# A grouped convolution with quantised weights: another order of loads, statistics and step sizes at the beginning

## The chip, the cores and the metric

The kernel runs on one core of a Trainium2 chip. The metric is the device time of one execution in microseconds (us); for each kernel several executions are timed and their median is compared. One execution is also recorded by the hardware profiler, and all lines of a profile come from that one.

## What is computed

The input `x` is 160 images of 128 channels by 32 x 32. Each image is normalised over groups of four channels, then convolved (3 x 3, padding 1, 128 channels to 128), and the result is added to the image itself. There are five weight sets; in the reference image m uses set m mod 5, and the kernel sorts the images so that it has 32 per set. The weights are quantised in two steps whose sizes come from the range of all five sets together:

```python
beta, alpha = jnp.max(U), jnp.min(U)
s1 = (beta - alpha) / 3.0
v1 = s1 * floor(U / s1)
s2 = s1 / 5.0
v2 = s2 * floor((U - v1) / s2)
w = (v1 + v2).reshape(128 * 5, 128, 3, 3)
act = conv_general_dilated(gn(x).reshape(32, 5 * 128, 32, 32), w, padding 1, feature_group_count=5)
out = x + act.reshape(160, 128, 32, 32)
```

So no weight can be quantised before all five sets have been read, and no convolution can start before the first weights are quantised.

## The kernel before

All channels lie on the 128 partitions. An image is split into a high and a low fp16 part (`high_part` L521, `low_part` L579), and TensorE multiplies both with the weights. The weights of a set are made in three columns (`make_column` L446), one for each horizontal tap, in the order 1, 0, 2 (`COLS`, L344); below they are the first, second and third column. The program is written out by hand: each engine runs its own instructions strictly in the order in which the Python code emits them, and waits at an instruction until what it reads is there.

The order of the beginning, in `run` (L774):

- **Loads** (L779 to L790), all issued by SyncE on one queue. Set 0 goes to `u0` in two halves of 288 KB, sets 1 to 4 go whole (576 KB) to `range1` to `range4`, image buffers that are given back after the range is known. Then follow images 0 to 3, one by one (512 KB, L414), and pairs of images (1024 KB, L411). The compiled program has eight landing counters for this queue and takes them in turn: its ninth transfer is issued once the first has landed, its eleventh once the third has, and so on.
- **Range** (`weight_range`, L420). VectorE takes the maximum (L426) and the minimum (L427) of each piece as it arrives, six pieces of 1, 1, 2, 2, 2 and 2 halves, then joins them (`ext1`, L431). `over_partitions` (L434) finds the extremes over the partitions: two transposes on TensorE (L439), a maximum on VectorE (`top`, L441) and a product with ones (`spread`, L443).
- **Step sizes** (`from_range`, L50): VectorE operations on 128 x 1 values. `span` (L74); `s1` by four operations (L58 to L61); four numbers from s1, called its parts (L66 to L71: minus s1, its reciprocal, and the two pieces of minus s1); `s2` by four operations from s1 (L58 to L61 again); `lift` (L78); the parts of s2. The loop at L832 puts them in turn with the operations of the first column: eight of these small ones come before the column's first operation, `nn` (L99), which needs the reciprocal of s1.
- **Columns**: thirteen operations on 128 x 384 values from `nn` to the second integer part (L112), then six products on TensorE that turn the column round (`pt`, L467), then ScalarE writes the weights (`wt`, L480). The second and the third column have their first operation on ScalarE (`ns`, L99).
- **Statistics** of images 0 and 1, and of 2 and 3, group by group. ScalarE sums an image (L192) and its squares (L199) into `mv`; TensorE averages over the channel group (`means`, L208); ScalarE copies (`ngm`, L217); four GpSimd operations make `dv` (L219 to L222); TensorE averages again (`variances`, L225); ScalarE (`ve`, L231) and GpSimd (L235 to L244) make `rstd` and `shift`, for which `lift` is needed (L239). Then ScalarE writes `z` (L515) and the high part `hi` (L523), and VectorE the low part `lo` (L581).
- **Dummy products** (`warm_up`, L636): products of zeros on TensorE, 14 between the means and the variances of images 2 and 3, and 7 after the first column's `pt`.
- **First three images**: TensorE takes the high parts of images 0, 1, 2 and then their low parts with the first column (L866 to L869: 36 products, L621). The second column's `pt` stands behind these 36 in TensorE's order. The 36 products with the second column follow, with the third column's `pt` among them, and then the third column.

The lines that set the order around the change:

```python
spread = self.over_partitions(self.weight_range(list(self.us.values())), ident)
...
for ahead in (8, 1, 1, 1, 1, 1, 3, 1, 1, 1):
    take(chain, ahead)
    take(first, 1)
run(chain)
measure(0, 0, 1)
measure(1, 0, 1)
self.stats[0].means()
```

Of the kernel before, what the change touches and what calls it, by code (L numbers as in the profile page):

```python
# [33 lines left out]
class Steps:  # L34
# [12 lines left out]
    def col(self, tag, dt=F32):  # L47
        return self.pool.tile([self.nc.NUM_PARTITIONS, 1], dt, tag=tag, name=tag)

    def from_range(self, extg):  # L50


        nc, col = self.nc, self.col

        def divide_exact(tag, q1, a, m):

            q0, rem = col(tag + "q0"), col(tag + "rem")
            yield nc.vector.tensor_scalar_mul(q0, a, 1.0 / m)  # L58
            yield nc.vector.scalar_tensor_tensor(rem, q0, -(m - 1.0), a, ALU.mult, ALU.add)
            yield nc.vector.tensor_sub(rem, rem, q0)  # L60
            yield nc.vector.scalar_tensor_tensor(q1, rem, 1.0 / m, q0, ALU.mult, ALU.add)  # L61

        def parts(out, s):

            r, neg, hi, lo = out
            yield nc.vector.tensor_scalar_mul(neg, s, -1.0)  # L66
            yield nc.vector.reciprocal(r, s)
            yield nc.vector.tensor_single_scalar(
                hi.bitcast(I32), neg.bitcast(I32), -4096, op=ALU.bitwise_and
            )  # L70
            yield nc.vector.tensor_sub(lo, neg, hi)  # L71

        span = col("span")
        yield nc.vector.tensor_reduce(span, extg, AX.X, ALU.add)  # L74
        yield from divide_exact("s1", self.s1, span, 3.0)
        yield from parts(self.parts1, self.s1)
        yield from divide_exact("s2", self.s2, self.s1, 5.0)
        yield nc.vector.tensor_scalar_mul(self.lift, self.s2, LIFT)  # L78
        yield from parts(self.parts2, self.s2)
        self.span, self.big = span, col("big")  # L80
        yield nc.vector.tensor_reduce(self.big, extg, AX.X, ALU.max)
# [51 lines left out]
def run(steps):  # L133

    while True:
        try:
            next(steps)
        except StopIteration as end:
            return end.value
# [107 lines left out]
def general_path(tc, keep, steps, x, u, out):  # L247
# [8 lines left out]
    with tc.If(far > 0), ExitStack() as ctx:  # L256
# [9 lines left out]
        for n in range(N_SETS):  # L266
            un = one.tile([P, C, TAPS], F32, tag="u", name=f"g_u{n}")
            nc.sync.dma_start(un, uv[n])
            wn = one.tile([P, C, TAPS], F32, tag="w", name=f"g_w{n}")
            k1, k2 = run(steps.quantise(one, un, f"g{n}", F32))  # L270
            nc.vector.tensor_scalar_mul(wn, k1, steps.s1)
            nc.vector.scalar_tensor_tensor(wn, k2, steps.s2, wn, ALU.mult, ALU.add)
# [37 lines left out]
class Main:  # L310
# [109 lines left out]
    def weight_range(self, us):  # L420

        nc, P = self.nc, self.P
        pieces = [us[0][:, : P // 2], us[0][:, P // 2 :], *us[1:]]
        ext = self.const.tile([P, 2, len(pieces)], F32, tag="ext", name="ext")
        for k, piece in enumerate(pieces):
            nc.vector.tensor_reduce(ext[:, 0, k : k + 1], piece, AX.XY, ALU.max)  # L426
            nc.vector.tensor_reduce(  # L427
                ext[:, 1, k : k + 1], piece, AX.XY, ALU.min, negate=True
            )
        ext1 = self.const.tile([P, 2], F32, tag="ext1", name="ext1")  # L430
        nc.vector.tensor_reduce(ext1, ext, AX.X, ALU.max)  # L431
        return ext1

    def over_partitions(self, ext1, ident):  # L434

        nc, P = self.nc, self.P
        rows = self.ps_tr.tile([1, 2, P], F32, tag="pt", name="rows")
        for k in range(2):
            nc.tensor.transpose(rows[:, k, :], ext1[:, k : k + 1], ident)  # L439
        top = self.const.tile([1, 2], F32, tag="top", name="top")  # L440
        nc.vector.tensor_reduce(top, rows, AX.X, ALU.max)  # L441
        spread = self.ps_tr.tile([P, 2], F32, tag="pt", name="spread")
        nc.tensor.matmul(spread, self.ones, top, start=True, stop=True)  # L443
        return spread
# [44 lines left out]
    def by_vector(self, i):  # L489
        return i in self.BY_VECTOR  # L490

    def measure(self, i, stages=(0, 1)):


        k = self.group_of[i]
        g = self.groups[k]
        if k not in self.stats:
            self.stats[k] = Statistics(
                self.nc, self.small, self.ps_stat, self.gavg, self.mhalf, len(g),
                self.steps.lift, k,  # L500
            )
        st, j, image = self.stats[k], i - g.start, self.image(i)
        if self.by_vector(i):
            st.image(j, image)
            return
        for s in stages:
            junk = self.unread.tile([self.P, 1024], MM, tag="junk", name=f"junk{i}_{s}")
            (st.image_sum, st.image_square)[s](j, image, junk)
# [265 lines left out]
    def run(self):  # L774
        nc, P = self.nc, self.P
# [3 lines left out]
        for n in range(N_SETS):  # L779
            if n == 0:  # L780
                un = self.upool.tile([P, P, TAPS], F32, tag="u", name="u0")
            else:
                un = self.space(f"range{n}").rearrange("p j e -> p (j e)")[:, : P * TAPS]
                un = un.rearrange("p (i k) -> p i k", k=TAPS)
            half = P // 2 if n == 0 else P
            for c in range(0, P, half):
                nc.sync.dma_start(un[:, c : c + half], self.uv[n][:, c : c + half])
            self.us[n] = un
        for c in range(6):
            self.load(c, single=c < 2)  # L790
        warm = self.const.tile([P, 1], F32, tag="warm", name="warm")
        nc.vector.memset(warm, 0.0)
# [1 line left out]
        ident = self.const.tile([P, P], F32, tag="ident", name="ident")  # L794
# [14 lines left out]

        self.ones = self.const.tile([1, P], F32, tag="ones", name="ones")  # L810
        nc.vector.memset(self.ones, 1.0)
        spread = self.over_partitions(self.weight_range(list(self.us.values())), ident)

        def take(steps, count):
            for _ in range(count):
                next(steps, None)

        def measure(stage, *images):
            for i in images:
                self.measure(i, (stage,))  # L820

        def parts(i):
            self.normalise(i)
            self.high_part(i)
# [3 lines left out]
        chain = self.steps.from_range(spread)  # L828
        first, second, third = (
            self.make_column(0, col, by_scalar=col != self.COLS[0]) for col in self.COLS  # L830
        )
        for ahead in (8, 1, 1, 1, 1, 1, 3, 1, 1, 1):  # L832
            take(chain, ahead)
            take(first, 1)
        run(chain)
        measure(0, 0, 1)
        measure(1, 0, 1)
        self.stats[0].means()
        self.stats[0].deviations()
        measure(0, 2, 3)  # L840
        self.stats[0].variances()
        self.stats[0].deviation()
        take(second, 1)
        measure(1, 2)
        self.stats[0].scales()
        measure(1, 3)
        self.stats[1].means()
        self.stats[1].deviations()
        self.warm_up(14)
        parts(0)  # L850
        self.stats[1].variances()
        self.stats[1].deviation()
        self.stats[1].scales()
        self.normalise(1)
        run(first)
        self.warm_up(7)
        self.high_part(1)
        parts(2)
        take(second, 2)
        self.low_part(0)  # L860
# [29 lines left out]
        for i in range(self.imgs):  # L890
            n, b = self.place(i)
# [13 lines left out]
            if i < self.FIRST:  # L905
# [3 lines left out]
                j = (i - 1) % self.FIRST  # L909
# [8 lines left out]
            else:  # L918
                j = i - 1
                self.conv(i, on_the_way)  # L920
            ahead = i + min(10 + i // 4, self.STAT_LEAD + 1)
# [27 lines left out]
            else:  # L949
# [18 lines left out]
                part = i + 3 < self.imgs and not self.combined(i + 3)  # L968
# [92 lines left out]
```

## Time and profile before

| what | value |
|---|---|
| median of five timed executions | 993.25 us (991.88 to 993.55) |
| the profiled execution: its own time, and its span | 993.7 us, 992.0 us |
| TensorE products busy | 957.7 us, 97% of the span |
| VectorE, ScalarE, GpSimd busy | 94%, 90%, 39% |
| share of the chain that ended last that lies on TensorE | 82% |
| first product with real weights (L621) starts | 32.17 us |
| first product with the second column's weights | 42.02 us |
| first product with the third column's weights | 50.89 us |

The span runs from the first to the last recorded instruction of the profiled execution. In a timeline a row has the start and the length in us, engine, line, operation, then output <- inputs; the square bracket tells how long the engine was idle before and on what it waited. The chain of waits is followed back from the last instruction: each row is what the next one had to wait for. PEld is the loading of weights into TensorE, SPq the queue of SyncE.

### The profile page before, as it was taken

To read this page: it belongs to the slowest core of one execution; us is meant where nothing else is said; L and a number is where in the kernel's file an instruction comes from. 1 tells how busy PE (TensorE), PEld (TensorE's weight loads), DVE (VectorE), ACT (ScalarE), POOL (GpSimd) and SP (SyncE) were. 2 spreads that over 40 slices of the span, in tenths; PEclk is the share of its full clock that TensorE was granted. 3 is DMA by queue.
4 is the path that set the end of the run, shared out by engine and by line. 5 is a ranking of instruction groups with operands and counts; after the bars stand their busy time and mean duration, and the time that the engine had idled before them with its cause. 6 is when DMAs were issued, how large, how long until landed. Compare 5 with 4: busy or idle time off the path is not lost.

```text
span 992.0 us, 16116 instructions
## 1 busy us (share of the span) xinstructions
PE 957.7 (97%) x5935; PEld 578.3 (58%) x5935; DVE 927.7 (94%) x1254; ACT 895.2 (90%) x1224; POOL 390.2 (39%) x565
## 2 busy tenths in 40 slices
PE   1999999999999999999999999999999999999997
PEld 0445665555666566666666566666665666666564
DVE  7999999999999999999999999999999998889995
ACT  3879999999999999999999999999999999998651
POOL 3524574733426253514262533315343424132410
PEclk9999999999999999999999999999999999999999
DMA  9528999999997999898989999998999898987764
GB/s 357 210 90 238 231 244 278 260 271 266 269 294 190 302 245 293 228 292 243 268 218 272 267 289 229 279 283 232 234 281 302 213 303 217 292 228 206 181 178 153
DMA packets 64985, 246.05 MB, mean 248 GB/s; under 512 B 4992, under 2 KB 4992, under 8 KB 64896
## 3 DMA queue, kind: packets, MB, share of 16 engines
q1 hardware_dynamic: 45168, 173.09, 50.1%
q0 software_dynamic: 19728, 71.84, 37.6%
q8 instruction: 48, 0.79, 0.3%
q14 instruction: 41, 0.34, 0.1%
HBM read 89.19 MB, written 83.89 MB: 174 GB/s over the span
## 4 chain that ended last, share of the span: by engine, by line
PE 82%; DVE 8%; ACT 4%; POOL 3%; issue 2%; DMA 1%; SPq 0%; DVEq 0%; POOLq 0%; ACTq 0%
PE eo L660 27%; PE m L660 27%; PE eo L621 26%; POOL v L546 1%; DVE eo L729 1%; ACT junk L199 1%; DVE eo L727 1%; DVE lo L581 1%; DVE vl L574 1%; ACT vh L568 1%; DVE v L557 1%; DMA range<-in_L_conv_U_dram 1%; PE m L641 1%; DVE ext L426 1%; DVE ext L427 1%
## 5 line engine op out<-in xcount | busy, mean ns | idle before, releaser
L660 PEld LDWEIGHTS <-wt 128*128 128x128 f16 x4266 | 417.2, 98 | 235.1 <-issue 6.9
L621 PE MATMUL eo<-hi,wt 128*128 128x496 f16 (+3 forms) x1422 | 339.6, 375 | 1.1 <-ACT wt L480 0.6
L765 POOL DMA_DIRECT2D xt<-sum x137 | 122.6, 901 | 458.7 <-ACT sum L746 444.1
L621 PEld LDWEIGHTS <-wt 128*128 128x128 f16 x1494 | 146.1, 99 | 142.6 <-ACT wt L480 1.9
L574 DVE SCALAR_TENSOR_TENSOR vl<-v,rstd,vh 128x2048 f16<-128x2048 f32 x80 | 188.1, 2352 | 4.1 <-ACT vh L568 4.1
L660 PE MATMUL m<-vh,wt 128*128 128x496 f16 (+1 forms) x480 | 182.2, 380 | 2.2 <-DVE eo L729 1.5
L660 PE MATMUL eo<-vh,wt 128*128 128x248 f16 (+1 forms) x960 | 183.9, 273 | 0.0
L660 PE MATMUL eo<-vl,wt 128*128 128x248 f16 (+1 forms) x960 | 183.9, 273 | 0.0
L660 PE MATMUL m<-vl,wt 128*128 128x496 f16 (+1 forms) x480 | 182.2, 380 | 0.2 <-DVE vl L574 0.2
L192 ACT ACTIVATE junk<-xt 128x1024 f16<-128x1024 f32 x152 | 160.6, 1057 | 17.8 <-DMA xt<-in_x_dram 14.1
L199 ACT ACTIVATE junk<-xt,mv 128x1024 f16<-128x1024 f32 x152 | 173.8, 1143 | 0.2
L568 ACT ACTIVATE vh<-v,rstd 128x2048 f16<-128x2048 f32 x80 | 160.8, 2010 | 2.5 <-POOL v L547 2.0
L746 ACT ACTIVATE sum<-eo 128x1024 f32<-128x1024 f32 x137 | 138.1, 1008 | 15.4 <-PE eo L660 15.3
L727 DVE TENSOR_TENSOR eo<-m,m 128x512 f32<-128x512 f32 x157 | 109.2, 696 | 35.8 <-ACT m L717 27.8
L660 PE MATMUL eo<-rows,wt 128*128 128x256 f16 (+1 forms) x924 | 138.9, 273 | 0.0
L660 PE MATMUL m<-rows,wt 128*128 128x496 f16 (+1 forms) x462 | 113.3, 380 | 0.3
L729 DVE TENSOR_TENSOR eo<-m,m 128x512 f32<-128x512 f32 x157 | 109.4, 697 | 3.6
L717 ACT COPY m<-m 128x512 f32<-128x512 f32 x157 | 90.5, 577 | 18.4 <-PE m L660 18.4
L515 ACT ACTIVATE z<-xt,shift,rstd 128x1024 f32<-128x1024 f32 x80 | 99.9, 1248 | 2.7 <-POOL shift L242 2.6
L581 DVE TENSOR_TENSOR lo<-z,hi 128x1024 f16<-128x1024 f32 x80 | 98.0, 1225 | 0.5 <-POOL shift L242 0.5
L557 DVE TENSOR_TENSOR v<-xt 128x960 f32<-128x960 f32 x80 | 91.9, 1148 | 0.0
L523 ACT CAST hi<-z 128x1024 f16<-128x1024 f32 x80 | 83.6, 1045 | 2.5
(111 smaller groups left out, 892.6 us busy)
## 6 DMA issues: line engine op xcount, KB each, us to landing
xt<-in_x_dram SPq DMA_DIRECT2D x78, 1024.0 KB, 9.6
out_dram<-xt SPq DMA_DIRECT2D x78, 1024.0 KB, 5.9
xt<-sum POOLq DMA_DIRECT2D x137, 512.0 KB, 6.1
range<-in_L_conv_U_dram SPq DMA_DIRECT2D x4, 576.0 KB, 7.9
u<-in_L_conv_U_dram SPq DMA_DIRECT2D x4, 576.0 KB, 9.1
xt<-in_x_dram SPq DMA_DIRECT2D x4, 512.0 KB, 10.0
out_dram<-xt SPq DMA_DIRECT2D x3, 512.0 KB, 2.9
u<-in_L_conv_U_dram SPq DMA_DIRECT2D x2, 288.0 KB, 3.0
```

Of the source, the lines that this page charges most:

```text
L192: self.nc.scalar.activation(junk, image, ACTF.Copy, scale=-1.0 / image.shape[1], accum_out=self.mv[:, j, 0:1],)
L199: self.nc.scalar.activation(junk, image, ACTF.Square, bias=self.mv[:, j, 0:1], accum_out=self.mv[:, j, 1:2],)
L557: nc.vector.tensor_sub(v[:, W:last], x[:, : last - W], x[:, 2 * W :])
L568: self.nc.scalar.mul(vh, self.v[i], st.rstd[:, j])
L574: self.nc.vector.scalar_tensor_tensor(vl, self.v[i], st.rstd[:, j], self.hi[i], ALU.mult, ALU.subtract)
L581: self.nc.vector.tensor_sub(lo[:, 1 : self.H + 1, :].rearrange("p h w -> p (h w)"), self.z.pop(i), self.hi[i].rearrange("p h w -> p (h w)"),)
L621: nc.tensor.matmul(self.bank(target, h)[:, r0 - h0 : r1 - h0, c0:c1], self.wts[n, col][:, k, :], tile[:, s0 : s0 + r1 - r0, c0 + dw : c1 + ...
L660: self.nc.tensor.matmul(target[:, :, c0:c1], self.wts[n, col][:, kind, :], source[:, :, c0 + dw : c1 + dw], start=start, stop=stop, skip_g ...
L727: nc.vector.tensor_add(rows[:, :, 0], m1, m2)
L729: nc.vector.tensor_sub(rows[:, :, 1], m1, m2)
L746: nc.scalar.mul(self.sum[i], eo.rearrange("p h r w -> p (h r w)"), 0.5)
L765: self.nc.gpsimd.dma_start(self.image(i), self.sum.pop(i), accum_op=ALU.add)
```

## The change

It touches only the beginning. The steady part of the program is the same, instruction for instruction.

- Set 1 is loaded in two halves as well, so the range has seven pieces (VectorE: two more operations, eight of 128 x 576 and six of 128 x 1152).
- Image 0 is loaded after set 2 and ahead of sets 3 and 4; image 1 stays behind all the sets.
- ScalarE measures image 0 wholly (sum, squares), then image 1. The means of this first group move on TensorE from behind `spread` to between the two transposes and `spread`.
- The four operations of s2 are put in turn with the parts of s1. Eleven small operations now come before `nn`; between the following steps of the first column stand two, one, one, one, one, one and one.
- ScalarE: `ns` of the second column goes from before the squares of image 2 to behind them; the high part of image 1 goes from behind the first column's `wt` to ahead of it.
- TensorE: 8 dummy products go between the variances of images 2 and 3 and the first column's `pt`, and 2 stay behind it (before: none and 7).

```diff
-        yield from parts(self.parts1, self.s1)
-        yield from divide_exact("s2", self.s2, self.s1, 5.0)
+        of_s1, s2 = parts(self.parts1, self.s1), divide_exact("s2", self.s2, self.s1, 5.0)
+        for chain in (s2, of_s1, of_s1, s2, of_s1, s2, s2, of_s1):
+            yield next(chain)
...
-        pieces = [us[0][:, : P // 2], us[0][:, P // 2 :], *us[1:]]
+        halved = [part for u in us[:2] for part in (u[:, : P // 2], u[:, P // 2 :])]
+        pieces = [*halved, *us[2:]]
...
-    def over_partitions(self, ext1, ident):
+    def over_partitions(self, ext1, ident, between):
...
             nc.tensor.transpose(rows[:, k, :], ext1[:, k : k + 1], ident)
+        between()
         top = self.const.tile([1, 2], F32, tag="top", name="top")
...
-            half = P // 2 if n == 0 else P
+            half = P // 2 if n < 2 else P
             for c in range(0, P, half):
                 nc.sync.dma_start(un[:, c : c + half], self.uv[n][:, c : c + half])
             self.us[n] = un
-        for c in range(6):
+            if n == 2:
+                self.chunks[0] = self.space("xt0")
+                nc.sync.dma_start(self.chunks[0][:, 0, :], self.xv[0, :, 0, :])
+        nc.sync.dma_start(self.chunks[0][:, 1, :], self.xv[0, :, 1, :])
+        for c in range(1, 6):
             self.load(c, single=c < 2)
...
-        spread = self.over_partitions(self.weight_range(list(self.us.values())), ident)
+        ext1 = self.weight_range(list(self.us.values()))
+        for i in range(2):
+            self.measure(i)
+        spread = self.over_partitions(ext1, ident, self.stats_of(0).means)
...
-        for ahead in (8, 1, 1, 1, 1, 1, 3, 1, 1, 1):
+        for ahead in (11, 2, 1, 1, 1, 1, 1, 1):
             take(chain, ahead)
             take(first, 1)
         run(chain)
-        measure(0, 0, 1)
-        measure(1, 0, 1)
-        self.stats[0].means()
         self.stats[0].deviations()
         measure(0, 2, 3)
         self.stats[0].variances()
         self.stats[0].deviation()
-        take(second, 1)
         measure(1, 2)
         self.stats[0].scales()
+        take(second, 1)
         measure(1, 3)
         self.stats[1].means()
         self.stats[1].deviations()
         self.warm_up(14)
         parts(0)
         self.stats[1].variances()
+        self.warm_up(8)
         self.stats[1].deviation()
         self.stats[1].scales()
-        self.normalise(1)
+        parts(1)
         run(first)
-        self.warm_up(7)
-        self.high_part(1)
+        self.warm_up(2)
         parts(2)
```

`stats_of(k)`, new, returns the statistics object of a group and makes it at its first use; `measure` did that itself before.

More of the change, by code (lines that the diff above doesn't have):

```diff
@@ L490, in by_vector, with stats_of @@
         return i in self.BY_VECTOR
+    def stats_of(self, k):
+        if k not in self.stats:
+            self.stats[k] = Statistics(
+                self.nc, self.small, self.ps_stat, self.gavg, self.mhalf, len(self.groups[k]),
+                self.steps.lift, k,
+            )
+        return self.stats[k]
     def measure(self, i, stages=(0, 1)):
@@ L496, in measure @@
         g = self.groups[k]
[L497 to L502, printed above, removed]
+        st, j, image = self.stats_of(k), i - g.start, self.image(i)
         if self.by_vector(i):
```

## The prediction

> **What bounds the kernel now.** The page first: TensorE is busy for 97% of the span, and cut into stretches of 100 us its products fill 99.7 us and more from 200 us to 900 us. So nothing that other engines do earlier or later counts there; the change can only move the moment from which TensorE is fed without a break. In this trace that is the second column's weights at 41.5 us, as the chain of waits shows for the first 42 us:
>
> ```profile
> 1.72 6.46 DMA range<-in_L_conv_U_dram
> ...
> 18.72 0.60 PE rows L439 x2
> ...
> 20.39 0.53 PE pg L208 x2
> 20.92 0.02 issue
> 20.95 0.17 ACT ngm L217
> ...
> 23.68 0.18 ACT ve L231
> ...
> 24.49 5.79 PE m L641 x14
> ...
> 33.50 1.25 ACT z L515
> 34.77 1.05 ACT hi L523
> ...
> 41.10 0.35 PE pt L467 x6
> 41.45 0.02 issue
> 41.48 0.49 ACT wt L480
> ```
>
> The reader is to see one rope: set 1 lands (8.18), VectorE takes extremes until 18.4, TensorE transposes, makes `spread` and only then the means of images 0 and 1 (20.4); from there statistics, 14 dummy products, statistics, image 2's high part (35.8), 24 products, `pt`. VectorE's timeline shows a second rope beside it, which matters as much:
>
> ```profile
> 5.75 0.74 DVE L427 TENSOR_REDUCE ext<-u 128x1 f32<-128x576 f32 x1
> 8.20 1.35 DVE L426 TENSOR_REDUCE ext<-range 128x1 f32<-128x1152 f32 x1 [1.71 <-DMA range<-in_L_conv_U_dram]
> ...
> 20.43 0.16 DVE L74 TENSOR_REDUCE span<-spread 128x1 f32<-128x2 f32 x1 [0.67 <-PE spread L443]
> ...
> 33.53 1.23 DVE L581 TENSOR_TENSOR lo<-z,hi 128x1024 f16<-128x1024 f32 x1 [0.50 <-POOL shift L242]
> ...
> 40.48 0.36 DVE L112 TENSOR_TENSOR k<-nn,lt 128x384 f16<-128x384 int16 x1
> ```
>
> It waits 1.71 us for set 1, later 0.50 us for image 1's high part, and ends the second column at 40.84; `pt` starts at 40.94. Both ropes end within 0.1 us, so the gain is the smaller of what the two gain. After `wt` at 41.48 ScalarE works without a gap until the third column's `wt` (50.36), so whatever is won at 41.5 is carried on whole.
>
> **Landings.** SyncE's rows tell them: the double image loads wait for the landing of sets 1 to 4 and start at 8.20, 9.64, 11.04 and 12.47. So a set lands every 1.42 us. ScalarE starts image 0 at 13.76 and image 1 at 15.10: an image takes 1.3 us.
>
> ```profile
> SPq L411 <- DMA range<-in_L_conv_U_dram: 3.6, 4, 1.0
> ...
> 12.47 0.37 SPq L411 DMA_DIRECT2D xt<-in_x_dram  x1
> ```
>
> **The change, step by step, against this execution (993.7 us).**
>
> 1. *Range.* A 128x576 reduction follows the last after 0.66 us, a 128x1152 one after 1.26. Halves cost VectorE 4 x 0.66 - 2 x 1.26 = 0.12 us more. When the first half of set 1 lands is not shown: not before u0's second half (issued at 1.25 and landed 3.1 later, 4.35), not after 8.18; I take the middle, 6.3, about where VectorE comes free (6.41). Second half at 8.2 to 9.55; set 2 lands at 9.6, reduced until 12.17; set 3 now lands behind image 0, 11.02 + 1.3 = 12.3; sets 3 and 4 take 5.04. L431 starts at 12.3 + 0.05 + 5.04 + 0.1 = 17.5 (0.05 from landing to start and 0.1 more after the last reduction, as here) instead of 18.41: **gain 0.9**. Ends: nothing gained if the half lands at 8.18 and set 3 a little later still; 1.77 if VectorE never waits (3.76 + 8 x 0.665 + 6 x 1.26 = 16.64). SyncE issues one transfer more (0.43 us) and image 1's now waits for u0's first half (3.7); both are hidden, since what is issued at 3.6 lands ten us later.
> 2. *Means ahead of `spread`.* The new wait on TensorE is for `mv` of images 0 and 1; behind it in the queue stand `spread` and so VectorE's whole second rope. Image 1 still lands at 15.1 (the same bytes lie ahead of it), its sum and squares take 2.4 us as at 16.29 to 18.80, so `mv` is there at 17.5. The transposes end at 18.4. The pair of product passes holds TensorE for 0.51 us (19.81 to 20.32), until 18.9, when `top` is ready. Cost 0.0 to 0.1; if `mv` came later than 18.4, one for one.
> 3. *Small operations.* A small operation starts 0.07 to 0.11 us after an unrelated one (21.43, 21.50, 21.61) and 0.19 after the one that it reads (20.62, 20.81, 21.00). Three more of them before `nn` make s1 to `nn` some 0.72 instead of 0.49; one more after `nn` costs 0.05; two fewer before `rest` give 0.07 back. The others stand between big operations whose distance is 0.65 with one (22.98 to 23.63) and without (27.21 to 27.86), so nothing. **Loss 0.2**, at least 0, at most 0.3.
> 4. *Statistics.* The means end at 18.9 instead of 20.9: the first rope gains 2.0 at once. `ve` then comes at 21.4, since ScalarE sums images 2 and 3 in 2.3 us between (before: 23.68). GpSimd's L239 needs `lift` too: VectorE has it at 22.4, GpSimd comes to it at about 22.7, so no wait; 0.3 later it would only shorten the idle time before `z`. The 14 dummy products start at 22.1 instead of 24.35 and end at about 28, `ve` of the second group follows at 28.2 (30.43). GpSimd needs 3.0 us from there to `shift` (30.43 to 33.46): `z` of image 2 at 31.3, its high part at 33.6. **The first rope gains 2.2.**
> 5. *`hi` of image 1 ahead of `wt`.* ScalarE: `z` 28.2, `hi` 29.5, `wt` 30.5, if `pt` is done. `pt` waits for the first column (28.8) and for the 8 new dummy products, which take 1.7 at the pace of the 7 old ones (1.67) or 3.4 at that of the 14 (0.42 each): 30.4 or 31.9. First real products at 31.1 or at latest 32.5. All 24 + 12 of them take 7.8, so they end at 39 to 40.4, which VectorE's 39.7 mostly hides. What this edit buys: image 1's `hi` is ready at 30.6, and VectorE's wait of 0.50 goes.
>
> Of the clock: the 14 dummies run 0.42 us apart, the products from 30.2 on at half that, 5.9 us after the first dummy; by this row the pace changes at 28. "TensorE: Matmul & The Clock Gate", Part 1, of the Trainium skill says that full clock comes after one busy window of about 3.4 us, which runs freely and so differs from run to run. By the page the change would come between 25.5 and 28.9, an estimate, and `pt` at 29 to 30.4: under VectorE's rope, so the sum would be the same.
>
> A rule against the change stands in "DMA: Bandwidth & Descriptors", Bandwidth: transfers of 1 MiB or more for good efficiency. If it held, the half would land nearer to 8.18 and step 1 would gain little. The rows with u0's halves (2 to 4 us) move 310 GB/s, those with whole sets (4 to 7 us) 304, so I take nothing off.
>
> *Sum.* VectorE's rope: 0.9 - 0.2 + 0.5, and 0.1 because the trace before ended on TensorE, 0.1 later: 1.3. TensorE's rope: 2.2. **The smaller one sets it: 993.7 - 1.3 = 992.4.** What is late next is VectorE with the second column; TensorE will idle before it for over 1 us. This execution lies 0.45 above the median of 993.25. Taken from the median, which is what is compared: **991.9**. The loads behind image 3, the stores and set 1's second load wait for buffers far ahead of use; they move with the rest.
>
> **Rivals** (0.2%, 2.0 us, is about what a measurement of this kernel can tell from no change).
>
> - *A, as above*: 0.9 to 1.9 us gained, 991.35 to 992.35. Chance 0.46.
> - *B, VectorE never waits for sets*: `ext1` 1.77 earlier; then `mv` (17.55) holds `spread` to 18.06, 1.75 earlier; less 0 to 0.2, plus 0.5: 2.05 to 2.4, 990.85 to 991.2. For it: from 4 to 8 us the queue moves 1.3 MB, two sets, while one is reported landed, so pieces may land earlier than my middle. Against it: set 2 would have to land 0.5 earlier than here. Chance 0.40.
> - *C, transfers are hidden anyway*: the half lands with the other at 8.2 and image 0 pushes set 3 past 13; step 1 gives 0 or loses 0.3 and `nn` is later: 992.5 to 993.5. Against it: the even 1.42 us. Chance 0.07.
> - *D, slower*: TensorE stays at the slow pace, since its work now begins earlier and with other pauses. Place: the dummies and the 36 first products, 0.42 us apart instead of 0.21. The products then start at 32.5 and end at 40.3 plus 0.21 for each slow one; before, they ended at 40.9. From four slow ones on the change is a loss, from 13 on one of 2.0; all 36 make it 7.0: 995.3 to 1000.2. Against it: 14 dummies sufficed, now there are 22 nearly in a row. Chance 0.07.
>
> So faster 0.42 (B and the edge of A), same 0.51 (A and C), slower 0.07. The range from 990.8 to 993.1 takes in A, B and most of C and leaves out D.
>
> **What will show it.** L431 at 17.5 (A), 16.7 (B) or 18.3 (C); `nn` 0.7 to 0.8 behind L61; means ahead of `spread` and no wait of `spread` on ScalarE; `ve` of the second group near 28.2; no wait of VectorE before image 1's `lo`; TensorE idle before the second column's `pt` with VectorE's L112 named; second column's `wt` at 40.2, the third's at 49.1. It would be wrong if `wt` came at 40.2 and the span still didn't shrink, or if L431 moved and the second column did not.

## The result, and the profile after

The changed kernel takes 991.87 us in the median (24 executions, 991.28 to 992.92), the kernel before 993.08 (44 executions, 991.43 to 994.4). The ratio is 0.9988, 95% interval 0.9983 to 0.9994: a gain of 1.2 us, within 0.6 to 1.7. Measured again later, beside three other kernels on one chip, the same kernel had 0.9982 (0.9973 to 0.9991), 1.8 us. The forecast was 991.9, range 990.8 to 993.1.

Its profiled execution took 992.99 us, span 991.2. The chain of waits of the changed kernel, for the first 40 us (start and length in us):

```profile
9.12 1.26 DVE ext L429
...
17.65 0.42 DVE top L446
18.07 0.04 issue
18.11 0.60 PE spread L448 x2
...
37.77 0.57 DVE lt L113
...
38.85 0.47 PE pt L472 x5
39.35 0.49 ACT wt L485
```

Where the chain before ran through statistics, dummies and TensorE's 24 products, it now runs through VectorE from 3.75 to 38.8, with only TensorE's transposes and `spread` between; the means (ahead of `spread` now) are not in it at all. VectorE's timeline has the details:

```profile
5.74 0.74 DVE L430 TENSOR_REDUCE ext<-u 128x1 f32<-128x576 f32 x1
6.40 0.74 DVE L429 TENSOR_REDUCE ext<-range 128x1 f32<-128x576 f32 x1
...
9.04 1.34 DVE L429 TENSOR_REDUCE ext<-range 128x1 f32<-128x1152 f32 x1
...
16.71 0.17 DVE L434 TENSOR_REDUCE ext<-ext 128x2 f32<-128x14 f32 x1
...
18.73 0.16 DVE L74 TENSOR_REDUCE span<-spread 128x1 f32<-128x2 f32 x1 [0.68 <-PE spread L448]
...
31.72 1.44 DVE L589 TENSOR_TENSOR lo<-z,hi 128x1024 f16<-128x1024 f32 x1
...
38.44 0.36 DVE L114 TENSOR_TENSOR k<-nn,lt 128x384 f16<-128x384 int16 x1
```

The first reduction on set 1 follows at 6.40 with no bracket: VectorE waited for no set at all. The join of the extremes is at 16.71, the wait for image 1's high part is gone (no bracket at 31.72), the second column ends at 38.80 (40.84), its `wt` starts at 39.35 (41.48). The join in the kernel before:

```profile
18.41 0.17 DVE L431 TENSOR_REDUCE ext<-ext 128x2 f32<-128x12 f32 x1
```

In the list of TensorE's waits the longest one after the start is the one forecast:

```profile
PE pt L472 <- DVE k L114: 1.9, 1, 1.9
```

**Where the 2.1 us went.** Matched copy by copy (ScalarE's copies of `m`, L717 before and L725 after, 157 of each), the changed execution leads by 2.12 us at 58 us and still by 2.08 at 718. At 720.7 its ScalarE waits 0.42 us for an image, from 724 on the copies lead by 1.77, and TensorE's last product starts 1.76 earlier (983.47 against 985.23). Then the end: from that start to the end of the span it is 7.7 us here and 6.75 before. In the second profile of the same kernel it is 6.7, and the lead is 2.30 us at its first copy and at its last, so both losses belong to one execution and not to the change. There the span is 989.6 and the execution's own time 991.4, against 993.7.

### The profile page after: what moved, and what is told of

It reads as the page before. It is cut to its first block, busy times and chain, and to the rows that moved or that the text cites. A ratio compares the mean times of both kernels' runs of the same rounds, so it can differ in the third digit from the quotient of the medians.

```text
span 991.2 us, 16124 instructions
## 1 busy us (share of the span) xinstructions
PE 957.9 (97%) x5938; PEld 578.1 (58%) x5938; DVE 928.3 (94%) x1256; ACT 895.4 (90%) x1224; POOL 386.7 (39%) x565
## 4 chain that ended last, share of the span: by engine, by line
PE 72%; DVE 12%; ACT 7%; issue 3%; POOL 3%; DMA 2%; SPq 0%; DVEq 0%; ACTq 0%; POOLq 0%
PE eo L668 24%; PE m L668 24%; PE eo L629 23%; ACT vh L576 2%; ACT junk L201 2%; DVE eo L737 1%; DVE eo L735 1%; DVE lo L589 1%; DMA xt<-in_x_dram 1%; DVE v L565 1%; POOL v L554 1%; ACT sum L754 1%; DVE vl L582 1%; ACT m L725 1%; DVE ext L429 1%
## 5 line engine op out<-in xcount | busy, mean ns | idle before, releaser
L725 ACT COPY m<-m 128x512 f32<-128x512 f32 x157 | 90.7, 578 | 18.4 <-PE m L668 18.4
```

## The experiments

Twelve runs, each beside the kernel before on the same chip. "Join" is VectorE's last reduction over the pieces, the next columns are the starts of the second and third column's `wt` on ScalarE; times in the profile in us.

| kernel | ratio to before, 95% interval | join | second | third |
|---|---|---|---|---|
| before (profile) | | 18.41 | 41.48 | 50.36 |
| changed (first profile) | 0.9988 (0.9983 to 0.9994) | 16.71 | 39.35 | 48.24 |
| changed, again | 0.9982 (0.9973 to 0.9991) | 16.56 | 39.18 | 48.07 |
| split of set 1 only | 0.9981 (0.9972 to 0.9990) | 17.06 | 39.55 | 48.44 |
| image 0 ahead only | 0.9998 (0.9989 to 1.0007) | 18.26 | 40.83 | 49.72 |
| order only | 0.9998 (0.9989 to 1.0007) | 18.41 | 41.03 | 49.92 |
| both loads only | 0.9982 (0.9973 to 0.9991) | 17.23 | 39.75 | 48.64 |
| 8 more dummies | 0.9982 (0.9973 to 0.9991) | 16.63 | 39.27 | 48.16 |
| image 2's low part later | 0.9985 (0.9976 to 0.9994) | 16.66 | 38.29 | 48.75 |
| and two of ScalarE's earlier | 0.9984 (0.9975 to 0.9993) | 16.80 | 38.42 | 48.88 |
| and its products last | 0.9989 (0.9980 to 0.9998) | 16.62 | 38.39 | 48.76 |
| set 1 by partitions | 1.0007 (0.9997 to 1.0016) | 19.50 | 42.28 | 51.16 |
| halves, reduced whole | 0.9993 (0.9984 to 1.0002) | 17.59 | 40.36 | 49.25 |
| all sets in halves | 0.9986 (0.9977 to 0.9996) | 16.63 | 39.13 | 48.03 |

**Taking the change apart.** Each kernel here is the kernel before with one part of the change. Set 1 in two halves and seven pieces, nothing else:

```diff
-        pieces = [us[0][:, : P // 2], us[0][:, P // 2 :], *us[1:]]
+        halved = [part for u in us[:2] for part in (u[:, : P // 2], u[:, P // 2 :])]
+        pieces = [*halved, *us[2:]]
...
-            half = P // 2 if n == 0 else P
+            half = P // 2 if n < 2 else P
```

> The kernel before with set 1 in two transfers and seven pieces, and nothing else of the change. Theory (two ropes, the smaller gain counts): both ropes hang on the range, so both are earlier by what the join of the extremes (L431 of before, 18.41) gains, and VectorE's 0.50 us wait for image 1's high part stays. If the order of the bytes sets the landings, set 2 lands at 9.6 as before, the join is at 17.2 and the time is 1.2 us less than before; if it is the halving that made the sets land 1.3 us sooner in the changed kernel, the join is at 16.7 and the time 1.7 less. Rival (the gain of the changed kernel comes from statistics and order, not from the loads): less than 0.3 us gained.

Measured: 1.9 us less (0.9981), no less than the whole change, join at 17.06, between the two joins that were foreseen. And VectorE does not wait for image 1's high part here either, against the expectation, so that the order is not needed for that.

Image 0 behind set 2, nothing else:

```diff
             self.us[n] = un
-        for c in range(6):
+            if n == 2:
+                self.chunks[0] = self.space("xt0")
+                nc.sync.dma_start(self.chunks[0][:, 0, :], self.xv[0, :, 0, :])
+        nc.sync.dma_start(self.chunks[0][:, 1, :], self.xv[0, :, 1, :])
+        for c in range(1, 6):
```

> The kernel before with image 0 loaded after set 2 and ahead of sets 3 and 4, and nothing else of the change. Theory (landings follow the order of the bytes): set 1 at 8.2, set 2 at 9.6, image 0 at 11, set 3 at 12.4, each in time for VectorE, which has them to reduce from 8.2 to 18.3 without a break: 0 us, within 0.3. Rival 1 (it is this order that lets sets land 1.3 us sooner): set 1 at 6.9, the join at 17.1, 1.3 us less than before. Rival 2 (set 3 is pushed too late): VectorE waits for set 3, up to 0.5 us more.

Measured: 0.9998, nothing that can be told from none; set 1 at 8.05. The landings do not hang on the image. The 0.65 us by which this profile's second column is earlier is no gain of the load: the join moved by 0.15, and TensorE's full pace came earlier after the first dummy than in the profile of before (below).

The order of the changed kernel with the loads and pieces of before (the two diffs above taken back):

> The changed kernel with the loads and the six pieces of before; step sizes, means, dummies and the order of ScalarE as changed. Theory: the join stays at 18.4; VectorE loses about 0.1 by the small operations and gains its wait of 0.50 for image 1's high part: 0.3 to 0.4 us less than before. TensorE's statistics rope gains some 0.9 (means no longer behind spread) but is not the one that decides. If landing times vary by chance from one execution to the next, set 1 lands in this profile somewhere else than at 8.18 and 6.87. Rival (statistics decide): 0.9 us less.

Measured: 0.9998; in the profile the second column's `wt` is 0.45 earlier, near the theory's figure and not the rival's 0.9. But the image alone, with the order of before, had 0.65, so this 0.45 shows no gain of the order. The timing cannot resolve 0.3 us. Set 1 landed at 8.2 again.

Both loads, order of before (both diffs):

> The kernel before with both changes of the loads (set 1 halved, image 0 ahead of set 3) and the order of before otherwise. Theory: the same as the split alone plus nothing for the image, join at 16.7 to 17.2, 1.2 to 1.7 us less than before; the sum of this and of the order alone (0.3) gives the 1.2 to 2.1 of the whole change. Rival (only together with the new order do the loads help, because the means hang on image 1): under 0.5 us.

Measured: 0.9982, join at 17.23. The rival is out: the loads need no new order.

**Which rope decides.** The changed kernel again:

> The changed kernel itself, beside the three others on one chip. So far the split of set 1 alone took 1.8 us off and both load changes alone 1.75, the whole change 1.2 and the order alone nothing. Theory (the order is worth nothing, the split is all): 1.2 to 1.8 us less than before, as the split alone. Rival (the new order costs some 0.5 us, which the split pays): 1.0 to 1.2. The profile should show sets land as in the other runs with the split, set 1 between 6.8 and 7.7, and the last stretch after TensorE's last product, 7.7 us in the first profile of this kernel against 6.7 in all others, back at 6.7.

Measured: 0.9982, and the stretch at the end 6.7 us. Neither a cost of the order nor a gain of it can be seen in the times. In the profiles the second column comes 0.2 to 0.4 earlier with it than with the split alone, but that is the join, which lies 0.35 and 0.50 earlier there. From the join to the second column's `wt` the table gives 22.49 with the split alone, 22.52 with both loads, 22.50 with all sets in halves, and 22.64 and 22.62 in the changed kernel: in these profiles the order costs some 0.1 us there. In the kernel before it is 23.07, with the wait of 0.50 in it.

The changed kernel with eight more dummies in front of the first real products:

```diff
-        self.warm_up(2)
+        self.warm_up(10)
```

> The changed kernel with 10 dummy products instead of 2 behind the first column's pt: 8 more, 1.7 us of TensorE just before the first real products. Theory (VectorE's rope decides, and TensorE idles 1.87 us before the second column's pt): those 1.7 us go into the idle time, 0 to 0.2 us more than the changed kernel. Rival (TensorE's rope decides): 1.7 us more than the changed kernel, that is slower than before.

Measured: 0.9982, the same as the changed kernel beside it. The timeline of TensorE in that kernel, and below it in the changed one:

```profile
30.48 2.70 PE L629 MATMUL eo<-hi,wt 128*128 128x512 f16 x12
...
38.77 0.46 PE L472 MATMUL pt<-ident,k 128*128 128x128 f16 x5 [0.46 <-DVE k L114]
```

```profile
29.03 2.71 PE L629 MATMUL eo<-hi,wt 128*128 128x512 f16 x12 [0.15 <-ACT wt L485]
...
38.85 0.46 PE L472 MATMUL pt<-ident,k 128*128 128x128 f16 x5 [1.87 <-DVE k L114]
```

The first real products start 1.45 us later than in the changed kernel (30.48, 29.03), the wait for VectorE shrinks from 1.87 to 0.46, and `pt` comes no later (38.77, 38.85). So TensorE's rope has that much slack and VectorE's decides. Shown.

**Why the halves land sooner.** These three are the kernel before with other loads. Set 1 in two transfers by partitions, with rows of full length:

```diff
+            if n == 1:
+                for p in (0, P // 2):
+                    nc.sync.dma_start(un[p : p + P // 2], self.uv[n][p : p + P // 2])
+                self.us[n] = un
+                continue
             half = P // 2 if n == 0 else P
```

> The kernel before with set 1 in two transfers by partitions, 64 each, so that its rows keep 4608 bytes; the extremes are taken of the whole set as before. It tells why the halves by columns let set 1 be whole at 6.8 to 7.7 where the one transfer lands at 8.1 to 8.2. Theory S (shorter rows, 2304 bytes): set 1 lands at 8.1 as before, the time is that of before. Theory N (two transfers and counters instead of one): set 1 lands at 6.8 to 7.7, the join is 0.5 to 1.3 us sooner and the time as much less.

Measured: later than one transfer. VectorE's first reduction on set 1, in this kernel (the next one's stands below):

```profile
9.29 1.35 DVE L426 TENSOR_REDUCE ext<-range 128x1 f32<-128x1152 f32 x1 [2.94 <-DMA range<-in_L_conv_U_dram]
```

Set 1 is whole at 9.2, the join at 19.50. Two transfers by themselves do not help; theory N is out. Theory S had 8.1 and the time of before: it did not foresee the loss of a whole microsecond in the landing either. The next kernel has two transfers by columns, but six pieces:

```diff
-            half = P // 2 if n == 0 else P
+            half = P // 2 if n < 2 else P
```

> The kernel before with set 1 in two transfers by columns, but with the extremes taken of the whole set when both have landed (six pieces). It parts the two ways in which the split can gain: earlier landing and earlier start of the reductions. Theory: landing at 6.8 to 7.7 gives 0.5 to 1.3 us (join at 17.1 to 17.9), and the rest of the 1.35 to 1.85 comes from the reductions that start on the first half. Rival (only the earlier start counts, the landing varies by chance): set 1 at 8.1, join at 18.4, nothing gained.

```profile
7.38 1.35 DVE L426 TENSOR_REDUCE ext<-range 128x1 f32<-128x1152 f32 x1 [0.98 <-DMA range<-in_L_conv_U_dram]
```

Measured: set 1 whole at 7.3, join 0.8 earlier, 0.9993 (its interval reaches 1.0002). So the split gains in two ways: in these profiles 0.8 us of the 1.35 by which the split alone moves the join come from the earlier landing, 0.5 from starting on the first half. (Its second column is compared with care only: VectorE waits 0.71 us ahead of image 2's low part here and with the set by partitions, and not with the split alone.) The queue as a whole need not be faster for it: from 4 to 7 us it moved 275 GB/s with the split alone, where set 1 was whole at 7.4, and 304 before.

All sets in halves:

```diff
-            half = P // 2 if n == 0 else P
+            half = P // 2
```

(with the seven pieces of the split.)

> The kernel before with all five sets in halves by columns; set 1 is reduced by halves, sets 2 to 4 whole. VectorE has no or little wait left with the split of set 1 alone (0.4 us), so theory: the join at 16.6 to 17.1, the time as with the split of set 1 alone, 1.5 to 2.0 less than before. What it tells of landings: theory S or N would have set 4 land earlier still than 11.7 (with one split) and 12.4 (with none), below 11.5; if the split only mends a delay at the very start, 11.7.

Measured: 0.9986, join at 16.63. SyncE's double image loads wait here for the halves of sets 3 and 4 and start at 9.03, 9.78, 10.53 and 11.27, so set 4 is there at 11.3, against 11.7 with one split and 12.4 with none. These landings go with the shorter rows, as theory S has it. But that rows of 2304 bytes *as such* do it was not tried apart from everything else (the halves read different stretches of memory too), and why halves by columns land sooner and halves by partitions later stays open.

**Can it be beaten?** If VectorE's rope decides, shortening it must help. The three kernels start from the changed one, and each of the last two diffs from the kernel ahead of it. The low part of image 2 goes behind the second column:

```diff
-        take(second, 2)
-        self.low_part(2)
...
-        for i in range(self.FIRST):
+        for i in range(self.FIRST - 1):
             self.direct_lo(i, self.COLS[0])
...
         run(second)
+        self.low_part(2)
+        self.direct_lo(2, self.COLS[0])
         measure(1, 5)
```

> The changed kernel with the low part of image 2 (VectorE, 1.14 us) and its six products behind the second column's quantisation instead of ahead of it. Nothing is left out. Theory (VectorE's rope to the second column decides): the second column's weights come 1.1 us sooner, at 38.2 instead of 39.35, and the time is 1.0 us less than the changed kernel. Rival (something else decides, ScalarE's or TensorE's order): 0, or more because the six products now lie behind the idle time.

And two operations of ScalarE earlier:

```diff
+        measure(1, 5)
+        measure(0, 6)
         run(second)
         self.low_part(2)
         self.direct_lo(2, self.COLS[0])
-        measure(1, 5)
         parts(3)
-        measure(0, 6, 7)
+        measure(0, 7)
```

> As the one before, and on ScalarE the squares of image 5 and the sum of image 6 (2.3 us) go ahead of the second column's weights, into the time in which ScalarE waits 3.7 us for pt. Theory (after the second column's weights ScalarE's unbroken row decides, until the third column's): the third column's weights come another 0.6 us sooner, where TensorE waited 0.61 for them, and the next wait, 0.59 for the statistics of images 4 to 7, shrinks: 1.6 to 2.2 us less than the changed kernel. Rival (TensorE's products decide from there on): nothing beyond the 1.0 of the one before.

And image 2's low products behind the second column:

```diff
         self.low_part(2)
-        self.direct_lo(2, self.COLS[0])
...
         for i in range(self.FIRST):
             self.direct_hi(i, self.COLS[1])
+            self.direct_lo(i, self.COLS[1])
             if i == self.FIRST - 1:
                 run(third)
-            self.direct_lo(i, self.COLS[1])
+        self.direct_lo(2, self.COLS[0])
```

> As the last one (low part of image 2 later, two operations of ScalarE earlier), but with image 2's six low products behind all products with the second column and behind the third column's pt. Theory (in the last one TensorE waited 0.7 us for that low part in front of the second column, and the third column's pt stood behind it): no such wait, second column's weights at 38.3 as there, third column's at 47.0 instead of 48.24 in the changed kernel, TensorE bridging the time by those six products: 0.6 to 1.2 us less than the changed kernel. Rival (the beginning no longer decides, or VectorE's total work does): third column's weights not before 48, 0 within 0.3.

Measured: all three bring the second column 0.9 to 1.1 us earlier, as expected, and the third 0.5 to 0.6 *later* than in the changed kernel (48.24); none is faster than it (0.9985, 0.9984, 0.9989 against 0.9988 and 0.9982). My reading after the first two, a wait for the low part, is only half of it: in the last one that wait is gone and the third column is no earlier. TensorE's timeline of the last one, products with the second column:

```profile
37.76 0.46 PE L472 MATMUL pt<-ident,k 128*128 128x128 f16 x5 [1.73 <-DVE k L114]
38.91 2.10 PE L629 MATMUL eo<-hi,wt 128*128 128x496 f16 x6 [0.69 <-ACT wt L485]
40.81 2.50 PE L629 MATMUL eo<-lo,wt 128*128 128x496 f16 x6
43.15 1.43 PE L629 MATMUL eo<-hi,wt 128*128 128x496 f16 x6
```

Six products take 1.43 us with their tail, and here 2.10 and 2.50. The table by stages has the reason (stage, length, TensorE's busy time and products, granted clock, DMA); first this kernel, then the changed one:

```profile
38.00:44.00 6.00, 5.31 (x21) 0.72 0.05 9
```

```profile
38.00:44.00 6.00, 4.57 (x25) 1.00 0.06 10
```

The granted clock fell: 1.7 us lost over some eight products at half pace. The third column was forecast at 47.0 and came at 48.76, so this loss is all that was missing. TensorE was idle from 36.0 to 37.8 and, but for 0.46 us of `pt`, on to 38.9. Dummies in that gap would be the next thing; that was not tried. No kernel here is faster than the changed one beyond the intervals.

## Why the prediction was right, step by step

- **What bounds it**: right. Two ropes, the second column's weights as the point where they meet, and the lead won there carried on until 718 us in one profile and to the end in the other.
- **Range** (0.9 forecast): right in mechanism, too small. The join gained 1.70 and 1.85 in the two profiles. The step that failed is "set 2 lands at 9.6": I kept the landings of before for everything ahead of image 0. Set 1 was whole at 6.9 (8.18), set 2 at 8.3, and image 1, put at 15.1, was there at 13.82. That is rival B's condition, and L431's reduction came at B's 16.7, not at A's 17.5; I had seen the sign for it, one set landed where the bytes of two had moved, and still put A first. SyncE's first load that waits for the whole of set 1, before and after:

```profile
8.20 0.38 SPq L411 DMA_DIRECT2D xt<-in_x_dram  x1
```

```profile
6.89 0.38 SPq L413 DMA_DIRECT2D xt<-in_x_dram  x1
```

- **Means ahead of `spread`** (0 to 0.1): right, 0. `top` was ready at 18.06 and `spread` started at 18.11.
- **Small operations** (loss 0.2): right. From s1 to `nn` it is 0.66 instead of 0.49, from `nn` to the end of the column 7.77 instead of 7.78: 0.17.
- **Statistics** (2.2): at least that. The means' copy came 3.1 earlier, `ve` of the second group at 26.17 (28.2 forecast), image 2's high part 4.25 earlier (30.52, 34.77). Part of that is the join, part TensorE's earlier full pace (below).
- **Image 1's high part ahead of `wt`** (0.5): the wait went, but it also goes without this edit, with the split alone and with both loads alone. With the image alone it was 0.15, and that execution's 14 dummies took 5.61 us where those of before took 5.93: before, TensorE's full pace came only with the last dummy, and the variances, `ve` and image 1's high part stand behind the dummies. A wait of 0.5 in one profile was priced as if it were in all. The dummies of before, of the image alone and of the changed kernel, and the wait with the image alone (this row names the high part, which is what the operation reads):

```profile
24.35 5.93 PE L641 MATMUL m<-lo 128*128 128x512 f16 x14
```

```profile
24.20 5.61 PE L641 MATMUL m<-lo 128*128 128x512 f16 x14
```

```profile
20.82 4.82 PE L649 MATMUL m<-lo 128*128 128x512 f16 x14
```

```profile
33.06 1.22 DVE L581 TENSOR_TENSOR lo<-z,hi 128x1024 f16<-128x1024 f32 x1 [0.15 <-ACT hi L523]
```

- **Sum**: 1.3 forecast; 2.1 at the second column in the profiles, 1.2 and 1.8 in the times. The profiled execution of before lay 0.6 above its median of 993.08; that a typical one starts its third column about so much earlier than 50.36 is argued from that, not shown. So that the number was met to the tenth is luck: two errors pulled against each other, the range sized too small and the wait of 0.5 too large. With the measured terms and no such wait the sum is 1.6 to 1.8.
- **Rivals**: what the profile shows is B's beginning with A's time. C and D did not happen. The slow pace that D feared did come in three later experiments, but not in D's place (the dummies and the 36 first products): TensorE fell back after it had idled before the second column.

On the clock: in the changed kernel the pace doubles 3.4 us after the first dummy (20.8 to 24.2: the 14 dummies take 4.82 us, eight of them 0.42 apart), where before it took 5.9. The profile's granted clock reads 1.00 in these stretches, so here only the distance of the products shows it. "TensorE: Matmul & The Clock Gate", Part 1, of the Trainium skill has freely running windows of about 3.4 us and a start that differs from run to run, and these rows agree. Its section "HAM oscillation" wants no idle gaps over some 3.4 us; the last experiment's row fell with gaps of 1.7 and 0.7 us, so here the measurement is stricter.

## What to carry to other kernels

Where the first reduction waits for a transfer, try that transfer in two halves and start on the first; here that one edit, by columns, held all of the gain that could be measured, and by partitions the join came 1.1 us later. Before moving work off the rope that decides, ask what the engine waiting at its end does with a longer gap ahead of it: TensorE lost in clock what it won in time. And a wait seen in one profile that hangs on the moment at which TensorE's pace changes is not a wait of every execution.

## What the runs showed of the hardware that was not expected

- One transfer of 576 KB with rows of 4608 bytes was whole at 8.05 to 8.2 us in three profiles; in two halves with rows of 2304 bytes it was at 6.7 to 7.7 in ten. Two halves with rows of 4608 bytes (64 partitions each) needed until 9.2, and the queue moved 209 GB/s from 4 to 7 us, against 304 before.
- TensorE's granted clock fell to half behind a stretch of 3.4 us with about 1.1 us of products in it (36.1 to 39.6 in the last experiment) and came back 3.4 us later. It did not fall in the changed kernel, which idles as long (1.87 and 0.58) at the same place, but after products that end later (37.0 instead of 36.0). There too a stretch of 3.4 us has only 0.95 us of products (36.8 to 40.2), so how full such a stretch is does not decide by itself.
